# Order within half chunks and fixed product banks, by eighths, in a two-layer relational graph network

## The chip, the cores and the metric

The kernel runs on one core of one Trainium2 chip. The metric is the device time of one execution in microseconds. The time before is the median of three timed runs. One more execution was taken with the hardware profiler, and all rows shown come from it.

## The reference

Two layers of a relational graph convolution over 50,000 nodes with 128 features, then a residual and a layer norm. There are 800,000 random edges and a loop on every node, sorted by destination, and 16 relations that are mixtures of 8 bases:

```
W   = einsum('rb,bio->rio', w_comp, basis)
agg = segment_sum(h[src], dst * 16 + rel)          # per node and relation
out = relu(einsum('nri,rio->no', agg, W) + h @ loop_w + bias)
...
x   = layernorm(x + layer2(layer1(x)))
```

## The kernel before

Everything is in float32. The kernel does not form the relations: it sums the weighted rows by node and basis, and multiplies by the 8 basis matrices afterwards.

**Tiles.** The real edges are cut into 6,250 tiles of 128 edges per layer, and ten tiles (`K`) make a chunk, of which there are `C` = 625. A chunk has two half chunks of five tiles (`PER`). For each tile:

- POOL gathers the 128 source rows from HBM by an indirect DMA (line 254, in `gather`) into one of four chunk buffers `g0` to `g3`. In program order the gathers of chunk c + 2 stand ahead of the matmuls of chunk c; a gather may only overwrite a tile's place once the matmul that read it, 40 tiles back, is done.
- DVE makes `hot` for a whole chunk (`hot_of`, lines 923 and 930): the weight of every edge for 8 bases, placed in one of 12 node columns (`WN`).
- PE multiplies the gathered rows by the tile's part of `hot`, 128 x 96 (line 1018). The five products of a half chunk go to one PSUM bank `pa`.
- DVE adds each product to `ring` (line 950), an accumulator in SBUF at an offset that is read from the edge list (`add`, with the offsets loaded into registers for two chunks at a time).

**Groups.** 512 nodes make a group. Ahead of its edges, `ring` is set to the loop's part: ACT copies the group's rows to a bank (`lay`, line 770), DVE multiplies them by a wide weight tile that SP loads (`own`, line 775). Behind its edges ACT copies the sums out of `ring` (`copy`, line 792), PE multiplies them by the bases and by the loop matrix (lines 798 and 803, in a bank `pn` of their own), ACT applies the bias and relu (line 810), PE turns the result back (`back`, line 822) and it is stored. Layer 2 adds x and normalises. Layer 1 also sorts the edges out, in steps between the chunks, and makes the edges' weights (line 668).

**Order.** PE, POOL, DVE and ACT run in the order in which the program is written. For a chunk and tile position `at` the loop writes the matmul, then the adds that are due, then other steps from a queue of events by due time (`go_on`). A matmul's add is put into the list `behind`, due `BEHIND` = 12 tiles later.

**Banks.** Eight PSUM banks: `fixed` (masks and bits), `pn`, and six that `Turns` hands out in rotation to products, lays, backs and the rest:

```
    def take(self, read=None):
        if len(self.held) == self.count:
            first = self.held.pop(0)
            if first is not None:
                first()                      # writes the reading steps of the oldest bank now
        self.held.append(read)
        return self.pool.tile([P, BANK], F32, name=self.name)
```

So a bank is taken only once the instructions that read its last content have been written, and the hardware waits are put in from the tile's reads and writes. The first add of a half chunk waits for all five matmuls of its bank, the later ones for the add before them.

Of the kernel before, what the change touches and what calls it, by code (L numbers as in the profile page):

```python
# [40 lines left out]
F32 = mybir.dt.float32  # L41
# [7 lines left out]
PSUM = bass.MemoryType.PSUM  # L49
# [29 lines left out]
AT_ONCE = 4  # L79
WIDE = 1  # L80
# [9 lines left out]
def tile_rgcn_resnorm(  # L90
# [130 lines left out]
    ps_a = ctx.enter_context(tc.tile_pool(name="ps_a", bufs=6, space=PSUM))  # L221
# [7 lines left out]
    class Turns:  # L229
        def __init__(self, pool, name, count):  # L230
            self.pool, self.name, self.count, self.held = pool, name, count, []

        def take(self, read=None):

            if len(self.held) == self.count:
                first = self.held.pop(0)
                if first is not None:
                    first()
            self.held.append(read)
            return self.pool.tile([P, BANK], F32, name=self.name)  # L240
# [10 lines left out]
    banks = Turns(ps_a, "pa", 6)  # L251
# [6 lines left out]
    def turned(h, m, sb):  # L258

        tp = ps_a.tile([P, BANK], F32, name="pa")  # L260
        nc.tensor.transpose(tp[:, :m], h, ident[:m, :m])
        hT = sb.tile([P, P], F32, name="hT")
        nc.scalar.copy(hT[:, :m], tp[:, :m])
        return hT[:, :m]
# [342 lines left out]
    def chunked():  # L607
        with (
# [20 lines left out]
            class Weights:  # L629
# [32 lines left out]
                def multiply(self):  # L662
                    m = self.m
                    self.po = [banks.take(self.keep) for _ in PARTS_OF]
                    for po, (j0, j1) in zip(self.po, PARTS_OF):
                        of = po[:, : 2 * AT * (j1 - j0) * NB].rearrange("e (n t w) -> e n t w", n=2, t=AT)
                        for j in range(j0, j1):
                            nc.tensor.matmul(  # L668
                                of[:, :, :, (j - j0) * NB : (j - j0 + 1) * NB],
                                self.is_rel[:m, j * P : (j + 1) * P],  # L670
                                each[:m],
                                start=True,
                                stop=True,
                            )
# [17 lines left out]
            class Group:  # L692
# [29 lines left out]
                def turn(self):  # L722
                    m = self.m
                    self.po = banks.take(self.keep)
                    for j in range(J):
                        nc.tensor.transpose(self.po[:, j * P : j * P + m], self.h[:m, j, :], ident[:m, :m])  # L726
# [14 lines left out]
                def combine(self):  # L741
                    self.comb = banks.take(self.combined)
# [174 lines left out]
            for n, of in enumerate((x, H1)):  # L917
# [79 lines left out]
                for c in range(C):  # L997
# [41 lines left out]
                banks.held = [None] * len(banks.held)  # L1039
            ordered.close()  # L1040

    def summed():
        L1 = dram.tile([N, D], F32, name="L1")
        L2 = dram.tile([N, D], F32, name="L2")
        with tc.tile_pool(name="io", bufs=2) as io, tc.tile_pool(name="sbf", bufs=2) as sb:
# [73 lines left out]
            def added(h, n, L):  # L1119


                def block(r0, p):
# [13 lines left out]
                    for e in range(ROW):  # L1136
# [4 lines left out]
                        for b in range(NB):  # L1141
                            if b % (BANK // D) == 0:
                                mb = ps_a.tile([P, BANK], F32, name="pa")
# [15 lines left out]
                        tp = ps_a.tile([P, BANK], F32, name="pa")  # L1159
# [83 lines left out]
```

## Time and profile before

| | |
|---|---|
| median of three timed runs | 18,209.43 us (18,202.78 to 18,209.78) |
| profiled execution, its own time | 18,065.77 us |
| its span, first to last instruction | 18,063.9 us |
| mean granted TensorE clock | 0.602 |
| busy: PE, weight loads, DVE, ACT, POOL | 46%, 35%, 36%, 9%, 66% |
| gathers of layer 1 | 6,250, from 47.9 to 9,070.3 us |
| gathers of layer 2 | 6,250, from 9,110.5 to 18,011.4 us |

In the rows, times are in microseconds unless marked ns. A group's row has line, engine, operation, tiles (written <- read), shapes and count, then busy time, mean ns of one, and the engine's idle time ahead of these instructions with what ended most of it. A row of waits has engine, line, what it waited for, and the total, the number and the longest. A timeline row has start, length, engine, line, operation, tiles, count, and in brackets the idle time ahead of it and its releaser; "issue" is time in which the profile shows nothing that was waited for, and "remote" an unknown queue. A row of a stretch has its bounds and length, the busy time (and number) of each engine listed, then granted clock, DMA share and GB/s. An fp32 matmul is two matmul records and two weight loads. PEld is the weight load, SP the engine that issues most DMAs.

### The profile page before, as it was taken

The page shows a single profiled execution, that of the slowest core. Times are in us where ns is not written, and L with a number is a line of the kernel's source. Part 1 is how long each engine was busy: PE and PEld are TensorE (multiplying, and loading weights), DVE is VectorE, ACT ScalarE, POOL GpSimd, SP SyncE. Part 2 cuts the span into 40 slices and gives each one's busy share as a digit, 9 for nine tenths or more (in the row PEclk, how much of TensorE's full clock was granted, in tenths as well). Part 3 has the DMA queues.
Part 4 walks back from the last instruction along what each step waited for, and adds up shares of the span by engine and source line. Part 5 has one row for each costly group of instructions (what it writes and reads, how often), then busy time and mean ns, then how long its engine had stood idle before and what let it go on. Part 6 is the DMA issues. An engine that isn't in the chain of part 4 may idle for free.

```text
span 18063.9 us, 132710 instructions
## 1 busy us (share of the span) xinstructions
PE 8315.7 (46%) x31484; PEld 6301.1 (35%) x31484; DVE 6563.7 (36%) x18253; ACT 1621.0 (9%) x2256; POOL 11861.6 (66%) x12540
## 2 busy tenths in 40 slices
PE   3444444444444444444444444444444444444444
PEld 2333333333333333333333333333333333333333
DVE  5444444443333333333333333333333333333333
ACT  0110011110100000010000000000000000000000
POOL 6666666666666666666666666666666666666665
PEclk7666666666666666666655555555555555555556
DMA  3333333333323322232322222222222222222222
GB/s 100 94 95 92 92 95 95 94 88 89 85 84 85 85 85 82 85 88 83 84 78 81 81 82 79 81 81 81 81 80 80 81 81 81 81 81 81 81 81 67
DMA packets 793018, 1527.32 MB, mean 85 GB/s; under 512 B 229924, under 2 KB 296342, under 8 KB 792230
## 3 DMA queue, kind: packets, MB, share of 16 engines
q0 software_dynamic: 403552, 826.82, 18.0%
q1 hardware_dynamic: 386934, 691.33, 11.6%
q8 instruction: 259, 4.24, 0.1%
q14 instruction: 529, 4.33, 0.1%
q10 hardware_dynamic: 1744, 0.60, 0.0%
HBM read 1390.97 MB, written 126.86 MB: 84 GB/s over the span
## 4 chain that ended last, share of the span: by engine, by line
issue 37%; PE 28%; another core or an unknown queue 16%; POOL 8%; DVE 5%; DMA 3%; ACT 1%; DVEq 1%; POOLq 0%; ACTq 0%; SPq 0%
PE pa L1018 18%; POOL g L254 8%; PE pn L798 8%; DVE ring L950 2%; DMA g<-H,src 2%; DVE ring L775 1%; PE pa L668 1%; PE pn L803 1%; DMA g<-in_x_dram,src 1%; ACT own L792 0%; PE pa L822 0%; DVE fixed L330 0%; DVEq L944 0%; DVE word L333 0%
## 5 line engine op out<-in xcount | busy, mean ns | idle before, releaser
L1018 PE MATMUL pa<-hot,g 128*128 128x96 f32 x25000 | 5704.8, 361 | 7613.1 <-issue 5607.3
L1018 PEld LDWEIGHTS pa<-hot,g 128*128 128x128 f32 x25000 | 5201.3, 276 | 9323.7 <-issue 7321.4
L254 POOL DMA_INDIRECT g<-in_x_dram,src x6250 | 5929.4, 949 | 3046.5 <-issue 1432.7
L254 POOL DMA_INDIRECT g<-H,src x6250 | 5895.2, 943 | 3045.9 <-issue 1428.8
L950 DVE TENSOR_TENSOR ring<-pa,ring 128x96 f32 x12500 | 3212.4, 257 | 10941.4 <-PE pa L1018 5215.2
L798 PE MATMUL pn<-own,basis 128*128 128x512 f32 x3104 | 2237.5, 799 | 508.1 <-issue 486.0
L930 DVE TENSOR_TENSOR hot<-pm,fixed 128x960 f32<-128x960 f32 x1250 | 1443.0, 1154 | 78.9 <-remote 19.2
L792 ACT COPY own<-ring 128x4096 f32<-128x4096 f32 x194 | 699.6, 3606 | 3172.0 <-DVE ring L950 2131.9
L775 DVE TENSOR_TENSOR ring<-wide,pa 128x2048 f32<-128x2048 f32 x392 | 893.7, 2280 | 84.1 <-issue 28.8
L798 PEld LDWEIGHTS pn<-own,basis 128*128 128x128 f32 x3104 | 656.1, 250 | 701.3 <-issue 696.3
L770 ACT COPY pa<-hT 128x512 f32<-128x512 f32 x392 | 230.8, 589 | 3035.4 <-DVE ring L950 1349.5
L726 PE MATMUL pa<-ident,rows 128*128 128x128 f32 x392 | 107.7, 420 | 829.6 <-ACT t L830 452.2
L810 ACT ACTIVATE oT<-pn,bias_of 128x512 f32<-128x512 f32 x196 | 134.3, 685 | 3928.0 <-PE pa L1018 2237.0
L668 PE MATMUL pa<-each,is_rel 128*128 128x128 f32 x1570 | 348.4, 377 | 291.8 <-issue 151.4
L668 PEld LDWEIGHTS pa<-each,is_rel 128*128 128x128 f32 x1570 | 300.5, 276 | 324.0 <-issue 226.2
L726 PEld LDWEIGHTS pa<-ident,rows 128*128 128x128 f32 x392 | 74.6, 223 | 845.1 <-ACT t L830 457.0
L923 DVE TENSOR_TENSOR fixed<-fixed,key 128x120 f32<-128x120 f32 x1250 | 350.4, 280 | 0.1
L822 PE MATMUL pa<-ident,oT 128*128 128x128 f32 (+1 forms) x784 | 218.6, 406 | 201.4 <-issue 133.9
L803 PE MATMUL pn<-hT,loop 128*128 128x512 f32 x392 | 263.1, 740 | 50.1 <-issue 49.9
L682 ACT COPY pm<-pa 128x192 f32<-128x192 f32 x628 | 141.0, 304 | 1063.8 <-remote 903.3
L822 PEld LDWEIGHTS pa<-ident,oT 128*128 128x128 f32 (+1 forms) x784 | 146.7, 219 | 230.2 <-issue 206.0
L597 ACT ACTIVATE sd<-mv,eps 128x4 f32<-128x4 f32 x98 | 29.1, 297 | 1929.9 <-DVE st L594 969.3
(129 smaller groups left out, 1655.8 us busy)
## 6 DMA issues: line engine op xcount, KB each, us to landing
wide<-CW SPq DMA_DIRECT2D x388, 1024.0 KB
g<-in_x_dram,src POOLq DMA_INDIRECT x6250
g<-H,src POOLq DMA_INDIRECT x6250
rows<-in_x_dram SPq DMA_DIRECT2D x194, 256.0 KB
PM<-pm SPq DMA_DIRECT2D x157, 160.0 KB
pm<-PM SPq DMA_DIRECT2D x157, 160.0 KB
H1T<-oT SPq DMA_DIRECT2D x97, 256.0 KB
H<-t SPq DMA_DIRECT2D x97, 256.0 KB
```

Source lines behind the costliest of these rows:

```text
L254: return nc.gpsimd.indirect_dma_start(out=to, out_offset=None, in_=of, in_offset=bass.IndirectOffsetOnAxis(ap=idx, axis=0))
L668: nc.tensor.matmul(of[:, :, :, (j - j0) * NB : (j - j0 + 1) * NB], self.is_rel[:m, j * P : (j + 1) * P], each[:m], start=True, stop=True,)
L770: nc.scalar.copy(self.laid[b][:, : self.cnt], self.hT[:, : self.cnt])
L775: nc.vector.tensor_tensor(ring[:, b : b + AT_ONCE, self.at : self.at + cnt], self.wide.pop(b)[:, :, :cnt], self.laid.pop(b)[:, None, :cnt] ...
L792: nc.scalar.copy(self.sums, ring[:, :, at : at + cnt])
L798: nc.tensor.matmul(self.pn[:, : self.cnt], BASIS[:, b, :], self.sums[:, b, :], start=b == 0, stop=False)
L803: nc.tensor.matmul(self.pn[:, : self.cnt], LOOP, self.hT[:, : self.cnt], start=False, stop=True)
L822: nc.tensor.transpose(self.po[:m, j * D : (j + 1) * D], by_place[:, j, :], ident)
L923: nc.vector.tensor_tensor(own[:, : ks(c)], grid[:, None, :].to_broadcast([P, ks(c), WN]), key[:, c * K : c * K + ks(c), None].to_broadcast ...
L930: nc.vector.tensor_tensor(hot[:, : ks(c)], pm[:, c % BATCH * K : c % BATCH * K + ks(c), :, None].to_broadcast([P, ks(c), NB, WN]), own[:, ...
L950: nc.vector.tensor_tensor(into, pa[:, k % PER * NB * WN : (k % PER + 1) * NB * WN].rearrange("d (b w) -> d b w", w=WN), into, op=OP.add,)
L1018: nc.tensor.matmul(pa[:, k % PER * NB * WN : (k % PER + 1) * NB * WN], g[:, k, :], hot[:, k].rearrange("e b w -> e (b w)"), start=True, st ...
```

## The change

Each layer's chunks are cut into eight sections of equal length (781 tiles). A table gives for each the number of banks that products rotate over, whether the five matmuls of a half chunk are written in reverse order, and whether their adds are. The last chunk of a layer is always forward. Layer 1 keeps six banks for all, and takes reversed products, adds or both in sections two, four, five, six and eight; layer 2 has 4, 4, 3, 2, 3, 2, 1, 4 banks, with products and adds reversed in the second, fifth, sixth and seventh. In layer 2 lays and backs rotate over banks 4 and 5 alone.

`Turns` gets six tiles that exist from the start in place of a pool, a turn for each set of banks, and for each bank the step that must be written before it is taken again. Adds of a section with reversed adds are put into `behind` in front of those of the same half, all with the due time of the half's last tile. The offsets are loaded when the pair of chunks changes, since the first add of a pair need not be its first tile.

```diff
@@ -77,6 +77,11 @@
 BEHIND = 12
 AFTER = 18
 AT_ONCE = 4
+SECTIONS = (
+    ((6, False, False), (6, True, True), (6, False, False), (6, True, False), (6, False, True), (6, True, True), (6, False, False), (6, True, True)),
+    ((4, False, False), (4, True, True), (3, False, False), (2, False, False), (3, True, True), (2, True, True), (1, True, True), (4, False, False)),
+)
+OTHERS = (None, (4, 5))
 WIDE = 1
 PARTS_OF = ((0, 3), (3, 5))
 EPS = 1e-5
@@ -218,7 +223,7 @@
                     left = less
             nc.vector.tensor_copy(split[:, n], mine)
 
-    ps_a = ctx.enter_context(tc.tile_pool(name="ps_a", bufs=6, space=PSUM))
+    ps_a = ctx.enter_context(tc.tile_pool(name="ps_a", bufs=1, space=PSUM))
     ps_f = ctx.enter_context(tc.tile_pool(name="ps_f", bufs=1, space=PSUM))
     fixed = ps_f.tile([P, BANK], F32, name="fixed")
     ps_n = ctx.enter_context(tc.tile_pool(name="ps_n", bufs=1, space=PSUM))
@@ -227,17 +232,18 @@
     nc.vector.tensor_copy(grid, col[:, :WN])
 
     class Turns:
-        def __init__(self, pool, name, count):
-            self.pool, self.name, self.count, self.held = pool, name, count, []
-
-        def take(self, read=None):
-
-            if len(self.held) == self.count:
-                first = self.held.pop(0)
-                if first is not None:
-                    first()
-            self.held.append(read)
-            return self.pool.tile([P, BANK], F32, name=self.name)
+        def __init__(self, tiles):
+            self.tiles, self.held, self.turn = tiles, [None] * len(tiles), {}
+
+        def take(self, read=None, among=None):
+
+            among = tuple(among or range(len(self.tiles)))
+            at = among[self.turn.get(among, 0) % len(among)]
+            self.turn[among] = self.turn.get(among, 0) + 1
+            if self.held[at] is not None:
+                self.held[at]()
+            self.held[at] = read
+            return self.tiles[at]
 
     class Once:
         def __init__(self, what, *args):
@@ -248,7 +254,7 @@
             if what is not None:
                 what(*self.args)
 
-    banks = Turns(ps_a, "pa", 6)
+    banks = Turns([ps_a.tile([P, BANK], F32, name=f"pa{i}") for i in range(6)])
 
     def gather(to, of, idx):
         return nc.gpsimd.indirect_dma_start(
@@ -257,7 +263,7 @@
 
     def turned(h, m, sb):
 
-        tp = ps_a.tile([P, BANK], F32, name="pa")
+        tp = banks.take()
         nc.tensor.transpose(tp[:, :m], h, ident[:m, :m])
         hT = sb.tile([P, P], F32, name="hT")
         nc.scalar.copy(hT[:, :m], tp[:, :m])
@@ -661,7 +667,7 @@
 
                 def multiply(self):
                     m = self.m
-                    self.po = [banks.take(self.keep) for _ in PARTS_OF]
+                    self.po = [banks.take(self.keep, OTHERS[0]) for _ in PARTS_OF]
                     for po, (j0, j1) in zip(self.po, PARTS_OF):
                         of = po[:, : 2 * AT * (j1 - j0) * NB].rearrange("e (n t w) -> e n t w", n=2, t=AT)
                         for j in range(j0, j1):
@@ -721,7 +727,7 @@
 
                 def turn(self):
                     m = self.m
-                    self.po = banks.take(self.keep)
+                    self.po = banks.take(self.keep, OTHERS[self.n])
                     for j in range(J):
                         nc.tensor.transpose(self.po[:, j * P : j * P + m], self.h[:m, j, :], ident[:m, :m])
 
@@ -739,7 +745,7 @@
                     )
 
                 def combine(self):
-                    self.comb = banks.take(self.combined)
+                    self.comb = banks.take(self.combined, OTHERS[0])
                     nc.tensor.matmul(
                         self.comb[: 2 * NB, : self.cnt],
                         split[:LOOPS].rearrange("r n b -> r (n b)"),
@@ -766,7 +772,7 @@
                     )
 
                 def lay(self, b):
-                    self.laid[b] = banks.take(self.owns[b])
+                    self.laid[b] = banks.take(self.owns[b], OTHERS[self.n])
                     nc.scalar.copy(self.laid[b][:, : self.cnt], self.hT[:, : self.cnt])
 
                 def own(self, b):
@@ -816,7 +822,7 @@
 
                 def back(self):
                     m = self.m
-                    self.po = banks.take(self.kept)
+                    self.po = banks.take(self.kept, OTHERS[self.n])
                     by_place = self.oT[:, : self.cnt].rearrange("o (p j) -> o j p", j=J)
                     for j in range(J):
                         nc.tensor.transpose(self.po[:m, j * D : (j + 1) * D], by_place[:, j, :], ident)
@@ -935,10 +941,13 @@
                     )
                     hots[c] = hot
 
+                pair = [None]
+
                 def add(c, k, pa):
 
                     i = c * K + k
-                    if i % (2 * K) == 0:
+                    if (n, i // (2 * K)) != pair[0]:
+                        pair[0] = n, i // (2 * K)
                         left = min(2, C - c) * K
                         offs = batches[c // BATCH].offs
                         nc.vector.load(at_reg[:left], offs[0:1, c % BATCH * K : c % BATCH * K + left])
@@ -1011,9 +1020,13 @@
                         if n == 0:
                             done(first_runs)
                     hot = hots.pop(c)
-                    for k in range(K):
-                        if k % PER == 0:
-                            pa = banks.take(Once(added_up_to, c * K + k + PER - 1))
+                    for at in range(K):
+                        part = SECTIONS[n][c * len(SECTIONS[n]) // C]
+                        k = at // PER * PER + (PER - 1 - at % PER if part[1] and c + 1 < C else at % PER)
+                        if at % PER == 0:
+                            pa = banks.take(
+                                Once(added_up_to, c * K + at + PER - 1), range(part[0])
+                            )
                         if k < ks(c):
                             nc.tensor.matmul(
                                 pa[:, k % PER * NB * WN : (k % PER + 1) * NB * WN],
@@ -1022,10 +1035,13 @@
                                 start=True,
                                 stop=True,
                             )
-                            behind.append((c * K + k + BEHIND, (c, k, pa)))
-                        added_up_to(c * K + k - BEHIND)
-                        if c or k == K - 1:
-                            go_on(c * K + k)
+                            if part[2] and c + 1 < C:
+                                behind.insert(len(behind) - at % PER, (c * K + at // PER * PER + PER - 1 + BEHIND, (c, k, pa)))
+                            else:
+                                behind.append((c * K + at + BEHIND, (c, k, pa)))
+                        added_up_to(c * K + at - BEHIND)
+                        if c or at == K - 1:
+                            go_on(c * K + at)
                     if n == 0 and c == 3:
                         beginning.close()
                     if n == 0 and c == C - 1:
@@ -1037,6 +1053,7 @@
                     go_on(now)
                     now += 1
                 banks.held = [None] * len(banks.held)
+                banks.turn.clear()
             ordered.close()
 
     def summed():
...
```

The rest of the diff takes two more banks of the fallback path `summed` (used only for inputs unlike these) from the same six tiles.

More of the change, by code (lines that the diff above doesn't have):

```diff
@@ L1142, in block @@
                             if b % (BANK // D) == 0:
-                                mb = ps_a.tile([P, BANK], F32, name="pa")
+                                mb = banks.take()
                                 nc.tensor.matmul(
@@ L1158, in block @@
                         at = tf[:p, e : e + 1]
-                        tp = ps_a.tile([P, BANK], F32, name="pa")
+                        tp = banks.take()
                         nc.tensor.transpose(tp[:p, :p], at.to_broadcast([p, p]), ident[:p, :p])
```

## The prediction

> **What bounds the kernel now.** I read the page first, then all instructions on the gather tiles, then the waits of POOL, then two stretches of the timeline, then busy time by stretch.
>
> ```profile
> PE 8315.7 (46%) x31484; PEld 6301.1 (35%) x31484; DVE 6563.7 (36%) x18253; ACT 1621.0 (9%) x2256; POOL 11861.6 (66%) x12540
> L1018 PE MATMUL pa<-hot,g 128*128 128x96 f32 x25000 | 5704.8, 361 | 7613.1 <-issue 5607.3
> L254 POOL DMA_INDIRECT g<-H,src x6250 | 5895.2, 943 | 3045.9 <-issue 1428.8
> ...
> L254 POOL DMA_INDIRECT g<-in_x_dram,src x6250: 938/944/1612, 47.9 to 9070.3; - x196
> L254 POOL DMA_INDIRECT g<-H,src x6250: 938/944/1022, 9110.5 to 18011.4; - x196
> ...
> 57.23 0.94 POOL L254 DMA_INDIRECT g<-in_x_dram,src  x1 [0.30 <-issue]
> 58.48 0.94 POOL L254 DMA_INDIRECT g<-in_x_dram,src  x1 [0.30 <-issue]
> ```
>
> No engine is full; POOL is nearest. A gather takes 0.94 us and the next cannot start for 0.30 us, also at the start of the kernel (last two rows) where nothing holds it: a floor of 1.249 us per tile, 7,806 us per layer. By the first and last start the gathers of layer 1 run 9,022 us and those of layer 2 8,901 us: 0.195 and 0.175 us per gather above the floor. These 1,216 and 1,095 us, and what starts and ends a layer, are all that a change of order or of banks can move, unless it adds waits. Who holds the gathers?
>
> ```profile
> POOL g L254 <- remote: 1603.5, 1256, 8.9
> POOL g L254 <- PE pa L1018: 1295.0, 1639, 8.3
> ...
> 12037.02 0.94 POOL L254 DMA_INDIRECT g<-H,src  x1 [2.65 <-remote]
> 12038.26 0.94 POOL L254 DMA_INDIRECT g<-H,src  x1 [0.31 <-issue]
> ...
> 12058.24 0.94 POOL L254 DMA_INDIRECT g<-H,src  x1 [0.30 <-PE pn L798]
> 12060.28 0.32 PE L1018 MATMUL pa<-hot,g 128*128 128x96 f32 x1 [1.07 <-issue]
> 12060.98 0.29 PEld L1018 LDWEIGHTS pa<-hot,g 128*128 128x128 f32 x1 [1.11 <-issue]
> 12061.00 1.13 DVE L950 TENSOR_TENSOR ring<-pa,ring 128x96 f32 x4 [14.57 <-remote]
> 12061.23 0.94 POOL L254 DMA_INDIRECT g<-H,src  x1 [2.05 <-remote]
> 12063.37 0.94 POOL L254 DMA_INDIRECT g<-H,src  x1 [1.20 <-PE pa L1018]
> 12065.24 5.94 PE L1018 MATMUL pa<-hot,g 128*128 128x96 f32 x33 [0.24 <-issue]
> 12065.51 0.94 POOL L254 DMA_INDIRECT g<-H,src  x1 [1.20 <-PE pn L803]
> 12066.75 0.95 POOL L254 DMA_INDIRECT g<-H,src  x1 [0.31 <-issue]
> ...
> 12087.02 0.94 POOL L254 DMA_INDIRECT g<-H,src  x1 [1.84 <-remote]
> 12094.07 0.94 POOL L254 DMA_INDIRECT g<-H,src  x1 [2.18 <-remote]
> ```
>
> Gathers run at 1.25 us for some 20 tiles, then wait, then run again. A gather overwrites the rows that the matmul of 40 tiles before has read (four buffers of ten tiles), so it waits for PE. At 12060.98 one step of PE lets go an add (12061.00) and a gather (12061.23) together. From 12037.02 to 12094.07 there are 40 gathers in 57.05 us, 7.1 us above the floor, in two rounds: some 3.55 us lost per 20 gathers, 0.177 each, as over the layer.
>
> Why is PE late, if its idle is only "issue"? Compare stretches, matmul records (two per tile) and weight loads:
>
> ```profile
> 9073.00:9079.00 6.00, 5.11 (x33) 4.90 (x32) 0.73 0.00 0
> 12045.00:12064.00 19.00, 2.56 (x8) 2.25 (x9) 0.61 0.19 48
> ...
> 9070.28 0.94 POOL L254 DMA_INDIRECT g<-in_x_dram,src  x1 [0.30 <-PE pa L1018]
> 9072.37 0.52 PE L1018 MATMUL pa<-hot,g 128*128 128x96 f32 x1 [1.09 <-issue]
> 9073.05 1.18 PE L1018 MATMUL pa<-hot,g 128*128 128x96 f32 x5 [0.17 <-issue]
> ```
>
> With 14 gathers running (12045 to 12064) PE does 8 records in 19 us; after the last gather of layer 1 it does 33 in 6 us. The steps in the slow stretch are 0.7 us apart (12060.28, 12060.98), 2.8 us for the four records of a tile, more than twice the floor. The fast one begins 1.83 us after that gather ended (9070.28 + 0.94 to 9073.05). So I read a see-saw: gathers slow PE, late PE stops the gathers, and once POOL has rested some 2 us PE clears its backlog and the gathers go on. What a stretch loses is (rest per round) / (tiles freed per round).
>
> **The change part by part.** An eighth is 781 gathers. Matmuls, adds and gathers keep their number; the rewritten bank pool adds no instruction. Waits go: the gather of a reversed half needs one PE wait for five tiles, which in the changed program's instruction order takes away some 5,000 separate semaphore instructions on POOL. I cost them at nothing: without them (57.23, 58.48) the spacing was 1.25 us too.
>
> *Products in reverse* (four eighths of layer 1, four of layer 2). The first gather of a half now waits for the matmul that stands last, so for all five, and the other four are then free. Reading it into the round above: POOL stops some four gathers sooner, but it makes one stop instead of three or four short ones (12061, 12063, 12065), and one stop is long enough to clear PE. A stop costs 2.0 us (1.83 us plus restart, less the ordinary 0.30; rows range from 1.54 to 2.35 when 0.30 is taken off). Ends: 2.0 per 20 gathers (0.10), and one stop per seven (0.29). I take 2.0 per 14, 0.143: 0.04 to 0.05 less than now. Rounded down for stops that do not clear PE: minus 30 us per eighth of layer 1 (-74 to +75), minus 25 us in the four-bank one.
>
> *Adds in reverse* alone (one eighth of layer 1): the five adds of a half read one bank and all wait for its fifth matmul already; 0.
>
> *Fixed banks in layer 2.* With B banks a half chunk waits for the adds of the half B before, so at most 5B tiles stand between PE and its adds; with six shared banks it was 30, or 25 while a lay or a back holds one. What is freed when POOL rests is the backlog, some 12 to 20 tiles, so four banks still hold it, three just, two and one not.
>
> ```profile
> 9073.13 1.43 DVE L950 TENSOR_TENSOR ring<-pa,ring 128x96 f32 x5 [2.96 <-remote]
> L930 DVE TENSOR_TENSOR hot<-pm,fixed 128x960 f32<-128x960 f32 x1250 | 1443.0, 1154 | 78.9 <-remote 19.2
> L775 DVE TENSOR_TENSOR ring<-wide,pa 128x2048 f32<-128x2048 f32 x392 | 893.7, 2280 | 84.1 <-issue 28.8
> L792 ACT COPY own<-ring 128x4096 f32<-128x4096 f32 x194 | 699.6, 3606 | 3172.0 <-DVE ring L950 2131.9
> ```
>
> - Four, forward (twice): 3.55 us per 18: +0.02, +20 us each (0 to 50).
> - Three, forward: 3.55 per 15 = 0.237: +48. Three, reversed: 2.0 per 12 = 0.167: -5.
> - Two, forward: 3.55 per 12 (ten and what trickles) = 0.296: +95 (20 to 250). Two, reversed: 2.0 per 10: +20 (0 to 200).
> - One, reversed: PE and DVE take turns. Per half: five matmuls (1.18 us for 2.5 tiles at 9073, so 2.4), five adds 1.43 and mostly a hot 1.15; about 5 us, which five gathers (6.25 us) cover. Then POOL must rest for every half: 2.0 per 5 = 0.40, +176. Once per 64 tiles the adds wait also for the copy to own (3.6 us) and the two products into the ring (2.28 each), which is past the cover: some 3 us in 64, +40. Together +215. Below: 0, if the turns hide. Above: if PE never leaves its 0.7 us steps, 14 us and 1.43 us per half, 3.1 us per tile, +1,310.
>
> Layer 1: -120. Layer 2: 40 - 25 + 48 - 5 + 95 + 20 + 215 = +388. Sum **+268 us**. The profiled execution took 18,065.8 us (span 18,063.9); by it the changed kernel takes 18,334. The timed median stands 0.8% higher, 18,209, and I add the same sum there: **18,477 us**.
>
> A place where the clock matters:
>
> ```profile
> 9110.00:18012.00 8902.00, 4261.17 (x14562) 3151.51 (x14563) 3066.31 (x8757) 702.10 (x861) 5894.86 (x6250) 0.58 0.28 81
> ```
>
> Layer 2 has a granted clock of 0.58 and 4,261 us of busy PE; at 0.5 the five eighths with three banks or fewer would take up to 5 x 533 x 0.16 = 426 us more of PE. I count none of it, because PE's steps in the slow stretch are 0.7 us whatever a matmul takes. The Trainium skill, "TensorE: Matmul & The Clock Gate", section "A second HAM failure mode: psum-queue depth-cycling", says that cycling through banks makes PE pause between groups until the clock gate falls back. By that rule the sum would be up to +694 us.
>
> **Rivals.**
> - *Much slower, one bank in slow steps.* POOL's rests let single steps of PE through and never clear it, so each half pays 14 us. For it: the 1.20 us stops at 12063 that ended without a burst. Against: reversed gathers rest until five tiles are done. It decides if a half takes over 10 us. +1,310 for the eighth and some 200 for the two-bank ones, less 40 elsewhere: about 19,650. Chance 0.08.
> - *Faster: the reversal outweighs the banks.* A round keeps its 19 tiles and pays one 2.0 us stop, 0.105. Layer 1: 4 x 781 x (0.195 - 0.105) = -280; four and three banks reversed -90; two banks 2.0 per 10 in both eighths, +40; one bank +176. Sum about -150, 18,060. For it: the one long stop before 12037.02 bought gathers without a stop up to 12058.24. Against: half a chunk of slack is given up. It decides if reversed eighths of layer 1 lose under 100 us. Chance 0.20.
> - *Hidden.* PE's slow steps are not the gathers' doing, so the windows matter only through PE plus DVE, 5 us per half against 7.1 now, and nothing changes: 18,209. For it: idle "issue" names no cause. Against: 33 records in 6 us begin as gathers end. The Trainium skill, "SBUF — State Buffer", section "Who interferes with whom", says that "PE and ACT never wait on anyone"; by that rule this rival holds, and the stretches at 9073 and 12045 speak against it. Chance 0.07.
>
> **How the numbers follow.** My forecast has 0.65, centred at 18,477, own range 18,250 to 18,900. About 0.2% (36 us) is what a measurement of this kernel tells from no change. Faster takes the second rival and a little of the forecast's lower tail, 0.22; same takes the third, 0.07; slower 0.71. The range goes from 18,000 (second rival with 60 us to spare) to 19,050 (two- and one-bank eighths at about half their upper ends) and leaves out the first rival and some tail on both sides.
>
> **What would show it.** Rate of gathers by eighth: in layer 1 the reversed ones shorter by some 30 us than forward ones; in layer 2 the eighth with one bank the longest, near 1.65 us per gather, with a stop of about 2 us every five; the forward two-bank one near 1.55; four banks as now. DVE's adds should follow PE at once in the last banks. Wrong if the one-bank eighth takes no longer than its neighbours, if reversed eighths are longer than forward ones, or if stops fall where PE is in a burst.

## The result, and the profile after

In 11 runs each, the changed kernel takes 18,163.76 us (18,153.82 to 18,173.97) and the kernel before, beside it, 18,202.78 us (18,189.99 to 18,212.08): ratio 0.9978, 95% interval 0.9970 to 0.9986, so 39 us less. The forecast was 268 us more. In two later comparisons the ratio was 0.9975 (0.9965 to 0.9985) and 0.9978 (0.9969 to 0.9987).

First a caution on levels. Each comparison below was made on one chip, with its own runs of the kernel before. That kernel took 18,203, 18,058, 18,187, 18,059 and 18,226 us in five of them and 15,805 us in one. The 15,805 us (e1 to e4) belong to a chip on which no other comparison ran; of the five others the second to the fourth ran on one chip, which so shows two levels 0.7% apart, the last on another, and the chip of the first is not on record. The profile of before shown in the prediction (18,065.8 us) belongs to a lower level than the profile of after (18,153.8 us), so the 88 us between these two profiles say nothing; only times of one comparison are set against each other, or it is said that they are not.

The page of the kernel after: busy times, and the groups of the product and of the two gathers.

```profile
PE 8241.1 (45%) x31484; PEld 6263.5 (35%) x31484; DVE 6617.4 (36%) x18253; ACT 1609.7 (9%) x2256; POOL 11892.4 (66%) x12540
...
L1031 PE MATMUL pa<-hot,g 128*128 128x96 f32 x25000 | 5598.0, 369 | 7929.0 <-issue 3815.2
...
L260 POOL DMA_INDIRECT g<-in_x_dram,src x6250 | 5944.2, 951 | 3082.2 <-issue 1519.6
L260 POOL DMA_INDIRECT g<-H,src x6250 | 5911.2, 946 | 3079.4 <-issue 1475.4
```

The picture is the old one: no engine full, POOL with 3,080 us of idle time per layer between its gathers. Then the gathers of layer 2 by eighth: bounds and length of the stretch, busy POOL and number, clock, DMA share, GB/s.

```profile
9145.80:10261.40 1115.60, 738.65 (x781) 0.57 0.27 81
10261.40:11379.00 1117.60, 738.75 (x781) 0.59 0.26 80
11379.00:12500.10 1121.10, 738.62 (x781) 0.58 0.26 80
12500.10:13620.50 1120.40, 738.64 (x781) 0.59 0.26 81
13620.50:14737.00 1116.50, 738.69 (x781) 0.60 0.26 81
14737.00:15855.70 1118.70, 738.73 (x781) 0.60 0.26 80
15855.70:16978.00 1122.30, 738.65 (x781) 0.59 0.26 80
16978.00:18100.50 1122.50, 740.48 (x783) 0.58 0.26 78
```

The eighths have 4, 4, 3, 2, 3, 2, 1 and 4 banks, and they take 1,115.6 to 1,122.5 us. The one-bank eighth, for which 1.65 us per gather was forecast, has 1,122.3 / 781 = 1.437; the forward two-bank one (the fourth, 1.55 forecast) has 1.435. So the windows, which carried most of the sum, cost next to nothing: the one-bank eighth takes 7 us more than the shortest. The stops did change shape. The waits of POOL in the seventh eighth of layer 1 (forward), then in the eighth one (reversed), then in the one-bank eighth of layer 2 (reversed): line, what was waited for, total, number, longest.

```profile
POOL g L260 <- PE pa L1031: 99.9, 105, 4.0
POOL g L260 <- remote: 91.9, 71, 4.2
...
POOL g L260 <- remote: 88.2, 35, 5.0
POOL g L260 <- PE pa L1031: 65.0, 26, 4.7
...
POOL g L260 <- remote: 154.8, 56, 4.7
POOL g L260 <- PE pa L1031: 13.8, 26, 1.4
```

Forward, 176 waits make 191.8 us; reversed, 61 make 153.2 us. Without the ordinary 0.30 us that any gather waits, that is 139.0 and 134.9 us. So there are far fewer and longer stops, as forecast, and nearly the same sum: 0.79 us per stop in the one and 2.21 in the other. The one-bank eighth has 82 such waits, not one per half chunk (156), and 168.6 us, 144.0 without the ordinary 0.30. A stop has no price of its own.

### The profile page after: what moved, and what is told of

It is laid out like the page before. It is cut to its first block, busy times and chain, and to the rows that moved or that the text cites. A ratio compares the mean times of both kernels' runs of the same rounds, so it can differ in the third digit from the quotient of the medians.

```text
span 18152.0 us, 126693 instructions
## 1 busy us (share of the span) xinstructions
PE 8241.1 (45%) x31484; PEld 6263.5 (35%) x31484; DVE 6617.4 (36%) x18253; ACT 1609.7 (9%) x2256; POOL 11892.4 (66%) x12540
## 4 chain that ended last, share of the span: by engine, by line
issue 22%; another core or an unknown queue 20%; PE 16%; DVE 9%; POOL 7%; DMA 1%; DVEq 1%; ACT 1%; POOLq 0%; SPq 0%; ACTq 0%
PE pa L1031 10%; POOL g L260 7%; DVE ring L959 5%; PE pn L804 5%; DVE ring L781 1%; DVEq L953 1%; DMA g<-in_x_dram,src 1%; DVE hot L936 1%; DMA g<-H,src 1%; PE pn L809 1%; DVE fixed L929 0%; PE pa L674 0%; ACT own L798 0%; DVE st L600 0%
## 5 line engine op out<-in xcount | busy, mean ns | idle before, releaser
L1031 PE MATMUL pa<-hot,g 128*128 128x96 f32 x25000 | 5598.0, 369 | 7929.0 <-issue 3815.2
L1031 PEld LDWEIGHTS pa<-hot,g 128*128 128x128 f32 x25000 | 5146.2, 281 | 9645.4 <-issue 5201.6
L674 PE MATMUL pa<-each,is_rel 128*128 128x128 f32 x1570 | 384.9, 389 | 600.6 <-DVE ring L959 302.9
L760 ACT COPY lrel<-pa 16x512 f32<-16x512 f32 x98 | 56.2, 574 | 1564.8 <-remote 677.3
L339 DVE COPY_PREDICATED word<-fixed,word 128x224 int32<-128x224 int32 (+9 forms) x450 | 178.4, 396 | 38.1 <-DVE fixed L336 11.5
```

Source lines behind the costliest of these rows:

```text
L674: nc.tensor.matmul(of[:, :, :, (j - j0) * NB : (j - j0 + 1) * NB], self.is_rel[:m, j * P : (j + 1) * P], each[:m], start=True, stop=True,)
L1031: nc.tensor.matmul(pa[:, k % PER * NB * WN : (k % PER + 1) * NB * WN], g[:, k, :], hot[:, k].rearrange("e b w -> e (b w)"), start=True, st ...
```

## The experiments

Two theories at first. R is the prediction's: each stop costs about 2 us, so the loss is 2 us over the tiles that a stop frees. S: each tile has some 0.18 us that can't lie beside a gather, however the stops are grouped.

**e1: the kernel before again.**

> The kernel before again, for a profile from the same chip as the other runs. Theory S (shared time: each tile needs about 0.18 us in which PE works and no gather is in progress, however the stops are grouped): its stops add up to 0.18 us per gather in both layers, as in the kernel after. Theory R (a price per stop, the one of the prediction: each stop costs about 2 us, so the loss is 2 us over the tiles that a stop frees): the same here. For both 18,200 us, and the profile of this run within 0.3% of it. If the profile again lies 0.8% below, the profiled executions can't be set against the medians.

15,804.6 us, and the runs of the kernel before beside it 15,805.3: some 2,400 us less than where the change was measured. Its gathers of layer 2 (shortest, median and longest in ns, first and last start):

```profile
L254 POOL DMA_INDIRECT g<-H,src x6250: 940/944/1013, 7966.3 to 15766.8; - x196
```

and a stretch of its timeline (start, length, engine, line, operation, tiles, number, idle time ahead and its releaser):

```profile
12050.49 1.17 PE L1018 MATMUL pa<-hot,g 128*128 128x96 f32 x4 [1.17 <-DMA g<-H,src]
...
12052.10 0.74 PE L1018 MATMUL pa<-hot,g 128*128 128x96 f32 x2 [0.45 <-DMA g<-H,src]
12053.27 0.94 POOL L254 DMA_INDIRECT g<-H,src  x1 [0.30 <-issue]
...
12054.52 0.94 POOL L254 DMA_INDIRECT g<-H,src  x1 [0.30 <-issue]
...
12055.86 0.74 PE L1018 MATMUL pa<-hot,g 128*128 128x96 f32 x2 [0.52 <-DMA g<-H,src]
12056.64 1.13 DVE L950 TENSOR_TENSOR ring<-pa,ring 128x96 f32 x4 [3.95 <-PE pa L1018]
```

Here layer 2 runs at (15,766.8 - 7,966.3) / 6,249 = 1.248 us per gather, the floor of the prediction. PE waits for each gather's data, not the gathers for PE, and the adds start at 12056.64, 0.04 us after the product before them ended (12055.86 + 0.74). So gathers don't make PE slow as such: the slow steps belong to the level (or the chip), not to the kernel.

**e2, e3, e4: at that same level.** The edits, each on the kernel after: every product issued twice; one bank in six eighths of layer 2; three buffers for gathered rows.

```diff
# e2: the nc.tensor.matmul(...) of the product written twice
# e3
-    ((4, False, False), (4, True, True), (3, False, False), ...),
+    ((4, False, False),) + ((1, False, False),) * 6 + ((4, False, False),),
# e4
-GATHERS = 4
+GATHERS = 3
```

> Every product of a tile is issued twice into the same place, so PE has twice the work per tile and the sums are unchanged. Theory S: the 0.18 us of PE per tile double, 0.36 us of stop per gather, +1,700 to +2,300 us. Theory R: a stop keeps its 2 us and grows only by the longer burst, 9 tiles of 0.22 us more per 16 gathers, 0.12 us per gather, +1,500 us. Rival H (PE's work is hidden, only the way its signals travel counts): no change, within 100 us of 18,160.

> In layer 2 the six middle eighths all have one bank, in forward order; layer 1 as in the kernel after. Theory R: rest of 2 us for every half chunk of five tiles, 0.40 us per gather against 0.18, over five eighths that had more banks 3,905 x 0.22 = +860 us, about 19,000. Theory S: the stops are only grouped differently, within 60 us of 18,164.

> Three buffers of ten tiles for the gathered rows instead of four, all else as in the kernel after: a gather waits for the matmul of 30 tiles before. Theory R: with PE 22 tiles behind, a stop frees some 8 tiles fewer, about 8 to 10 per stop instead of 16, 0.2 to 0.25 us per gather in place of 0.18 even with shorter stops and up to 0.37 with stops as long as now: +250 to +2,300 us. Theory S: stops twice as frequent and half as long, the same sum, within 60 us of 18,164.

15,810.0, 15,811.4 and 15,820.9 us against 15,805.3, ratios 1.0003, 1.0003 and 1.0010, whose intervals all reach 1. With the gathers at the floor no theory is tried, except that PE with twice the products still keeps up.

**e5: one bank in six eighths, again.**

> The kernel with six one-bank eighths in layer 2 once more, since its first run and the kernel before beside it took 15,805 us, with the gathers at their floor, and so say nothing of the 18,200 us that the kernel before takes where its matmuls run late. If the kernel before takes 18,200 us here: theory R +860 us; theory S within 60 us of the kernel after, 18,164. If it takes 15,805 us again, equal to it within 10 us by every theory, since the gathers never wait for PE.

This time the kernel before took 18,057.5 us; one bank 18,062.6, ratio 1.0003 (0.9993 to 1.0013). R wanted some 860 us more. The six eighths together:

```profile
10189.30:16882.20 6692.90, 4419.73 (x4686) 0.59 0.28 81
```

6,692.9 / 4,686 = 1.428 us per gather, with PE and DVE taking turns on one bank. R falls here. (This kernel keeps layer 1's part of the change, so a cost of some tens of us may be hidden by a gain there; see e16.)

**e6 to e9: the change again, and PE's part of the loss**, in one comparison, where the kernel before took 18,186.9 us. e6 is the kernel after; e7 and e8 are the edits of e2 and e4; in e9 two of five products are left out:

```diff
+                            if k % PER % 2 == 0:
                                 nc.tensor.matmul(
...
-    pa[:, k % PER * NB * WN : (k % PER + 1) * NB * WN]               # read by the add
+    pa[:, k % PER // 2 * 2 * NB * WN : (k % PER // 2 * 2 + 1) * NB * WN]
```

> The kernel after once more, for the size of its gain beside the kernel before. Where the kernel before takes 18,000 us or more: 39 us less (0.2%) if the gain belongs to the change, 0 if it was one comparison's own. Where it takes 15,805 us: the same within 10 us.

> Every product issued twice, as before, now hopefully where the matmuls run late. Theory S (PE's work of a tile and the gathers exclude each other, 0.18 us per tile): +1,700 to +2,300 us. Theory E (what limits is the rate at which completions are passed on, some 1.43 us for all that belong to one tile, whatever PE's work between them): within 100 us of the kernel after. Where the kernel before takes 15,805 us: no change by either.

> Three buffers of gathered rows instead of four, again. Theories S and E: a limit on throughput, so within 60 us of the kernel after. A theory L (each gather waits out a fixed lateness of PE, so a shorter way ahead costs in proportion): 30 tiles instead of 40 in the same lateness of some 57 us, 57/30 = 1.9 us per gather in place of 1.43, +5,900 us. Where the kernel before takes 15,805 us: no change, +15 us as measured before.

> Two of every five products are left out (the adds of their tiles read the neighbour's product, so DVE's work and all gathers stay). Theory S: 0.4 x 0.18 us less per gather, -900 us. Theory E: only the completions of those matmuls go, one in twenty or so of a tile's, at most -400 us. Where the kernel before takes 15,805 us: no change.

The results are 18,143.6 (ratio 0.9975), 18,427.3, 18,153.3 and 17,994.2 us, those of e7 and e9 from two runs each. The gain of the change is there again, 43 us. Three buffers cost 10 us against e6, inside the noise: how far POOL may run ahead does not matter either, which ends R a second time, and L. Doubled products cost 284 us, far from the 1,700 of S, and 40% fewer products gain 149 us, far from 900: S falls. E has the better numbers (at most 100 and at most -400), but 284 us is more than it allowed. The profile's pages give a hint on what these two have in common. The first line of that of e7:

```profile
span 18423.6 us, 176687 instructions
```

and of e9:

```profile
span 17984.3 us, 104204 instructions
```

e6 has 126,693 recorded instructions, e7 49,994 more, e9 22,489 fewer: 5.7 and 6.6 ns for each. The kernel before has 6,017 more than after (132,710), and takes 43 us more: 7.2 ns. Hence theory T: where matmuls run late, each instruction costs some 6.6 ns, whatever it does. (e7 and e9 change PE's work together with the count, so by themselves they don't tell the two apart.)

How late the signals are is seen in e6's timeline, in an eighth of layer 2 with three banks:

```profile
12056.59 1.86 PE L1031 MATMUL pa<-hot,g 128*128 128x96 f32 x8
12057.80 0.95 POOL L260 DMA_INDIRECT g<-H,src  x1 [0.30 <-issue]
...
12069.05 0.94 POOL L260 DMA_INDIRECT g<-H,src  x1 [0.30 <-issue]
12070.56 1.43 DVE L959 TENSOR_TENSOR ring<-pa,ring 128x96 f32 x5 [14.03 <-remote]
12070.80 0.94 POOL L260 DMA_INDIRECT g<-H,src  x1 [0.80 <-remote]
...
12072.05 2.02 PE L1031 MATMUL pa<-hot,g 128*128 128x96 f32 x8 [13.60 <-issue]
...
12075.70 0.94 POOL L260 DMA_INDIRECT g<-H,src  x1 [3.96 <-remote]
```

The products of a half chunk end at 12058.45 (12056.59 + 1.86). DVE is idle, yet their five adds start only at 12070.56, 12.1 us later, just when POOL has stopped, against 0.04 us in e1. PE in turn waits for those adds, until 12072.05. So PE is not slow at its work: its finished work is reported late while gathers run, and a report comes through as POOL pauses.

That the report is late, and not DVE, is in the same trace. The products raise a semaphore, a counter that other engines wait for, and the trace keeps when it rose: in e6 at 12070.54, and the first add began 0.02 us behind; in e1 at 12056.61, 0.01 us after the product's end, and the add again 0.02 us behind. From 500 us behind the first gather on, it rose 0.47 times per us within e6's gathers and 1.67 times per us in gaps of over 0.6 us between them; in e1 1.05 times per us within gathers. Nor is the lateness a fixed delay. From the end of a half chunk's products to its first add, the medians of e6's eighths of layer 2 are 18.6, 19.3, 15.8, 8.5, 17.7, 8.7, 1.2 and 17.7 us, for 4, 4, 3, 2, 3, 2, 1 and 4 banks, while the eighths take the same time within 7 us; in e1 no eighth has a median above 0.4 us. Fewer banks let fewer half chunks stand in line, and each stands there for less time. That is how a line behaves that is served at a fixed rate, as in E; what serves it no run shows.

**e10 to e13: instructions, or the order?** One comparison, the kernel before at 18,058.8 us. e10 and e11 fold more of POOL's waits together, e12 adds idle work on ScalarE to the kernel after, e13 has layer 2's part alone. P is T for PE and POOL only, W a gain by reversal itself.

```diff
# e10, both layers
+    ((6, True, True),) * 8,        # and OTHERS = (None, None)
# e11, beside that
-    k = at // PER * PER + (PER - 1 - at % PER if part[1] and c + 1 < C else at % PER)
+    k = K - 1 - at if part[1] and c + 1 < C else at
# e12
                         added_up_to(c * K + at - BEHIND)
+                        for _ in range(2):
+                            nc.scalar.copy(idle[:, 0:1], idle[:, 1:2])
# e13, layer 1
+    ((6, False, False),) * 8,
```

> All sixteen eighths with products and adds in reverse, six banks everywhere and no bank kept for the other work: 5,000 instructions fewer on POOL than the kernel after, 5,200 in all. Theories T (6.6 ns for every instruction, where matmuls run late) and P (for those of PE and POOL alone): 33 us below the kernel after, some 77 us below the kernel before, ratio 0.9958. Theory W (reversal by itself brings it, by the number of reversed eighths: 39 us for seven with products in reverse): some 90 us below the kernel before. If banks brought it: equal to the kernel before. Where the kernel before takes 15,805 us: equal within 15 us.

> As the run with all eighths reversed, but the ten products of a chunk run from last to first, not each half's five: POOL waits for PE once per ten gathers, 6,200 instructions fewer on POOL than the kernel after, 6,400 in all. T and P: 42 us below the kernel after, 85 below the kernel before, ratio 0.9953. Theory R would have one stop per ten tiles free ten at once and lose less, but has fallen. Where the kernel before takes 15,805 us: equal within 15 us.

> The kernel after with two copies of one number a partition on ScalarE behind every product, 25,000 in all, into a tile that nobody else reads: 24,600 instructions more on ScalarE. ScalarE is busy 9% of the time, and the copies add some 0.2 us each, 5,000 us, beside the rest. T: +162 us over the kernel after. P: 0. If they hold up the copies to own and with them the adds: some tens of us by either. Where the kernel before takes 15,805 us: 0.

> Layer 1 as in the kernel before (six banks, all forward), layer 2 as in the kernel after: half of the removed instructions come back. T and P: 17 to 20 us above the kernel after, 26 below the kernel before, ratio 0.9986. If the fixed banks of layer 2 cost what the reversal of layer 1 gains: at or above the kernel before.

- e10: 17,991.6 us, ratio 0.9963 (0.9949 to 0.9976), -67 us; T said -77, W -90. It has the lowest ratio of the complete kernels, though it did not run beside the kernel after, whose intervals overlap with its own.
- e11: 18,012.6 us, 0.9973 (0.9963 to 0.9984), -46 us where T said -85. Folding further, with 1,245 instructions fewer than e10, brought nothing more. The traces show what became of the stops. The kernel before, in the profile of 18,066 us, has 1,393 gathers that start over 1.6 us after the one before, on average 1.58 us above the 1.249 us; e10 has 683 of 3.21 us, e11 585 of 3.78 us. All that the gathers lose to the floor in both layers is 2,313, 2,241 and 2,260 us (not of one comparison). Half the stops, twice as long, lose nearly the same.
- e12: 18,120.6 us, 1.0032 (1.0020 to 1.0044), +62 us above the kernel before, although its POOL and PE have fewer instructions than that kernel's, as after. P, and any story of order alone, wanted some 40 us below. T wanted +162 over the kernel after, +120 over before. By count it is half T's rate: 62 us for 18,547 more (151,257 against 132,710) is 3.3 ns. But ScalarE is waited for, and two rows of e12's waits are put down to the new copies:

```profile
DVE ring L961 <- ACT idle L1046: 150.0, 37, 15.5
PEld pa L1033 <- ACT idle L1046: 94.9, 56, 13.7
```

Adds stood still for 150 us in all behind them, and the expectation gave such holding up some tens of us. So e12 shows that work on ScalarE costs time here; how much of it is a price per instruction it does not show.
- e13: 18,055.6 us, 0.9997 (0.9988 to 1.0006), -3 us where T said -26 (the interval goes from -22 to +11 us).

**e14 to e17: the parts side by side.** The kernel before at 18,226.5 us.

```diff
# e16: layer 2
+    ((6, False, False),) * 8,
+OTHERS = (None, None)
# e17: layer 1, and layer 2's reversals with six banks
+    ((6, False, False),) * 8,
+    ((6, False, False), (6, True, True), (6, False, False), (6, False, False), (6, True, True), ...),
+OTHERS = (None, None)
```

> The kernel before, for a profile by layer beside the next three. Where matmuls run late: layer 1 some 9,020 to 9,100 us from the first gather to the last, layer 2 some 8,900 to 8,960 us, at 18,050 to 18,200 us.

> The kernel after a third time, beside its parts. 39 to 43 us below the kernel before if both earlier comparisons hold on this chip too; less if the gain belongs to the chip on which they were made.

> Layer 1 as in the kernel after, layer 2 as in the kernel before (six banks, all forward). T (6.6 ns for each of some 3,000 instructions fewer): 20 us below the kernel before, and half of the whole change's gain. If layer 2's part gains nothing, as its run alone says: as far below as the whole change, some 40 us. By the prediction's terms 120 us below.

> Layer 1 as before; in layer 2 the same eighths reversed as in the kernel after, but six banks throughout and none kept for the other work. T: 20 us below the kernel before. If the fixed banks cost what the reversals gain: 20 us or more below the kernel before and below the run of layer 2's part alone (3 us below). If reversal in layer 2 gains nothing: 0.

e15, the whole change: 18,185.3 us, -41 us. e16, layer 1's part: 18,192.9 us, 0.9984 (0.9975 to 0.9993), -34 us (between -46 and -13). e17, layer 2's reversals without fixed banks: 18,211.2 us, 0.9991 (0.9982 to 1.0000), -15 us. So layer 1 brings most of the gain, by these medians. Layer 2's reversals bring some 15 us of their own, at the edge of what is measured, and with the fixed banks 3 us (e13, in another comparison); the intervals of e13 and e17 overlap, so a cost of the fixed banks is not shown. Stretches of gathers, of e14 and then of e15: the eighths with reversed products of layer 1 (second, fourth, sixth, eighth), then the sixth and seventh of layer 2 (reversed, two banks and one).

```profile
1201.10:2346.60 1145.50, 740.84 (x781) 0.61 0.31 91
3482.30:4641.20 1158.90, 741.60 (x781) 0.61 0.31 90
5766.40:6895.90 1129.50, 737.75 (x781) 0.61 0.29 84
8025.80:9156.90 1131.10, 739.38 (x783) 0.62 0.29 84
14806.00:15931.90 1125.90, 736.57 (x781) 0.59 0.28 80
15931.90:17055.10 1123.20, 736.63 (x781) 0.58 0.27 80
sum 6814.10, POOL 4432.77; mean POOL 738.80
```

```profile
1202.70:2340.00 1137.30, 745.57 (x781) 0.62 0.31 92
3486.80:4630.00 1143.20, 743.01 (x781) 0.61 0.32 92
5755.30:6880.80 1125.50, 738.99 (x781) 0.62 0.29 84
8007.30:9132.90 1125.60, 740.72 (x783) 0.62 0.29 84
14770.90:15888.10 1117.20, 737.39 (x781) 0.60 0.28 81
15888.10:17010.30 1122.20, 737.46 (x781) 0.59 0.27 80
sum 6771.00, POOL 4443.15; mean POOL 740.52
```

And the gathers of both layers, of e14:

```profile
L255 POOL DMA_INDIRECT g<-in_x_dram,src x6250: 938/944/1584, 48.1 to 9155.9; - x196
L255 POOL DMA_INDIRECT g<-H,src x6250: 938/944/1010, 9195.3 to 18178.9; - x196
```

and of e15:

```profile
L260 POOL DMA_INDIRECT g<-in_x_dram,src x6250: 938/945/1612, 47.8 to 9131.9; - x196
L260 POOL DMA_INDIRECT g<-H,src x6250: 938/945/962, 9169.0 to 18135.2; - x196
```

The six stretches lose 43.1 us (6,814.1 to 6,771.0), about the whole difference of the two spans, 18,230.5 to 18,187.6. The reversed eighths of layer 1 lose 8.2, 15.7, 4.0 and 5.5 us, the two-bank one of layer 2 8.7 us, the one-bank one 1.0 us. The rest nets out: the other four eighths of layer 1 grow by 9.7 us and the other six of layer 2 shrink by 7.7. The same code differs by up to 5.7 us per eighth from one profile to the next (layer 1 of e14 and e17), so the sums say more than single eighths. With e16 and e17 there are two profiles of each form of layer 1: the means of the four reversed eighths fall by 31.8 us in all, those of the other four rise by 4.4.

## Why the prediction was wrong

- **The bound.** Right, for the level it was read at: the gathers' floor of 1.249 us is what the kernel runs at in e1, and the time above it is POOL's waits. That this loss belongs to the kernel was wrong: at 15,805 us it is absent, with the same instructions.
- **"A see-saw: gathers slow PE".** Half right. Reports come through faster when POOL pauses (1.67 rises per us against 0.47 in e6). But "PE steps" were read as PE working slowly. In e6 a half chunk's products ran within 1.86 us, and its adds started 12.1 us after their end.
- **"(rest per round) / (tiles freed per round)" with 2.0 us per stop.** This is the step that failed: a stop was given a fixed price (2.0 us, or 3.55 us per round of forward eighths), and every term but the adds' 0 and the +40 for the copies to `own` stood on it. A stop has no fixed length. Where one frees five tiles there are fewer and longer ones (61 of 2.21 us against 176 of 0.79), with half as many they are twice as long (e10), one bank stops 82 times and not 156, and a shorter way ahead costs 10 us in all (e8): the loss per gather stays. The prediction's own rows of POOL's waits held a warning: 2,895 waits (1,256 and 1,639) of 1.0 us on average, 0.7 without the ordinary 0.30, while the 2.0 came from the long stops of one stretch. The fixed price put layer 2 at +388 us and layer 1 at -120. In the rows of e14 and e15 above, layer 1 goes from 9,107.8 to 9,084.1 us, -24, and layer 2 from 8,983.6 to 8,966.2, -17 (first to last start of a gather).
- **Products in reverse, -30 per eighth of layer 1.** The sign held, the size was about a quarter: -33 us in four eighths. The reason given (one long stop clears PE) is not needed. The 5,000 waits that I "cost at nothing", because a gather without them had the same 1.25 us spacing, are what may remain: they go with the reversed eighths, and at this level the time goes with the number of instructions (e7, e9, e10). That they are the cause was not shown, as no run took them away and kept the order. T's 20 us for e16 and e17 and 77 for e10 lie within what was measured, its 26 for e13, 85 for e11 and 120 for e12 do not.
- **Adds in reverse alone: 0.** The fifth eighth of layer 1 had 1,125.2 us of gathers in e14 and 1,125.3 in e15, by the bounds of the stretches above (4641.20 to 5766.40 and 4630.00 to 5755.30).
- **One bank, +215, two banks +95 and +20.** Within 10 us of their neighbours in the profile after. The kernel with six eighths of one bank (e5) was 5 us slower in all; set against the 34 us that layer 1's part gained in e16, another comparison, its banks cost at most some 40 us, 6 to 7 us per eighth. That one bank holds up so little, although PE and DVE take turns, fits this: a half chunk has 5 x 1.43 = 7.1 us, PE and DVE need the 5 us that I counted for it, and the report of the products, which has no other half chunk ahead of it, takes 1.2 us at the median.
- **What would show it.** The sign "wrong if the one-bank eighth takes no longer than its neighbours" came true: it took 1,122.3 us beside 1,118.7 and 1,122.5. So did one that was meant to confirm: the adds follow PE more closely in the last banks (1.2 us against some 18 with four). It did not bring the cost that was hung on it.
- **The clock, up to +426 us, and the Trainium skill's page "TensorE: Matmul & The Clock Gate", section "A second HAM failure mode: psum-queue depth-cycling".** The page tells of a kernel in which cycling through banks made PE pause and its clock swing. No run here shows that: the granted clock in the one-bank eighth is 0.59, in the four-bank ones 0.57 to 0.59.
- **The rivals.** "Faster", chance 0.20, had the sign, at -150 us, by the same fixed price of a stop. "Hidden", 0.07, was nearest in time: PE plus DVE did fit into what a half chunk takes now. That PE's lateness is not the gathers' doing, which it supposed, stays half open: PE's signals come more slowly within gathers than between them, but gathers alone don't make them late (e1). What the Trainium skill's page "SBUF — State Buffer" says in "Who interferes with whom", that PE waits on no one, is a rule on the use of SBUF; the 1.86 us that e6's products took agrees with it, and of their signals it says nothing.
- **Much slower** was to decide from 10 us per half chunk. In the one-bank eighth a half chunk takes 5 x 1.437 = 7.2 us.

What stays open: what makes the reports late at all. At 6.6 ns, all 126,693 instructions of the kernel after would make 836 us, and its excess over 15,805 us is some 2,360. The rest may lie in the gathers' own completions; no run took those away. Why one comparison of six had no lateness is not known; it was the only one on its chip. One difference stands in the traces: for the same kernel that of e1 keeps 259,966 rises of semaphores, those at the upper level 56,008 (before) and 54,694 (e14). Either rises were handed on several at a time, or some were not recorded. With this goes a rival that no run excludes. Every time on record comes with a span and a granted clock of its execution, and a price per instruction on whichever engine, like a semaphore that rises late, could also come from the recording of events.

## What to carry to other kernels

Before a wait is given a price per occurrence, find out whether its sum is conserved: one run with a shorter way ahead (three buffers for four) or with one bank would have shown that regrouping the stops moves the time by a few tenths of a per cent at most. The mean of all waits, beside the few that a timeline shows, is the cheapest test. Set profiles against each other only within one comparison, since the same kernel stood at 15,805 and at 18,226 us. Turning the order round, so that one wait stands for five, was worth 0.2 to 0.4% here where signals ran late.

## What the runs showed of the hardware that was not expected

| against, in the same comparison | instructions | time | ns for each |
|---|---|---|---|
| e7 against e6 (products twice) | +49,994 | +284 us | 5.7 |
| e9 against e6 (two of five left out) | -22,489 | -149 us | 6.6 |
| e12 against before (ScalarE) | +18,547 | +62 us | 3.3 |
| e10, e11 against before | -11,204, -12,449 | -67, -46 us | 6.0, 3.7 |
| after against before, three times | -6,017 | -39, -43, -41 us | 6.5 to 7.2 |
| e16, e17 against before | -2,957, -3,168 | -34, -15 us | 11, 4.8 |
| e13, e5 against before (fixed banks) | -3,421, -3,545 | -3, +5 us | 0.9, none |

The count is the page's number of recorded instructions. Where PE's reports are late, the time goes with it at 3 to 7 ns in most runs. That the count itself is the cause is not shown: e7 and e9 change PE's work too, e10 and e11 the stops, and in e12 others wait for ScalarE. The rows of e13, e16 and e17 have intervals of some 16 us to either side. At 15,805 us there is none of it: e2, with 43,977 more instructions than the kernel before, takes 5 us more. And the report of a finished half chunk let the adds start 0.04 us after its end in e1 and 12.1 us after it in e6; with one bank in place of four the median of that time fell from 18 to 1.2 us, and the gathers were no faster.
